# Cross attention with an adapter on one core: other ranks and other weights for changes of tiling in a build-time scheduler

## The chip, the core and the metric

The kernel runs on one core of a Trainium2 chip, in fp32. The metric is the time of one execution on the device in microseconds, smaller being better; a kernel's time is the median of its runs. Five engines work side by side, each through its own instructions in program order: TensorE (PE in the profile; PEld are its weight loads), VectorE (DVE), ScalarE (ACT), GpSimd (POOL) and SyncE (SP), which here issues the DMAs. They wait for each other by semaphores.

## The reference, cut to what matters

The inputs are x (2, 2048, 640) and a context (2, 128, 384). There are 8 heads of width 80. The last 4 tokens of the context belong to the adapter, the other 124 are text.

```python
query = hidden_states @ Wq                       # 2 x 2048 rows
keyt, valt = enc @ Wk, enc @ Wv                  # enc: 124 text tokens
hs = _mha(query, keyt, valt)
ca_q1 = jnp.einsum('btc,th->bch', ca, Wq_ca)     # 384 rows, from 4 tokens
ca_q1 = ca_q1[:, indices, :]                     # 2048 rows, each one of the 384
ca_hs1 = _mha(ca_q1, residual, residual)         # residual is x
ca_q2 = ca_hs1 @ Wq
ca_hs2 = _mha(ca_q2, ca @ Wk_ca, ca @ Wv_ca)
out = (hs + ca_hs2) @ Wout + b_out + residual
```

`_mha` is softmax attention with a scale of d ** -0.5. As the rows of ca_q1 repeat, everything behind them up to ca_hs2 is computed for 384 rows and gathered by index at the end.

## The kernel before, in words

**How it is issued.** Every part of the work is a Python generator (a task) that yields steps, `Do(engine, fn, after, needs, frees, marks, rank, mode)`: an engine or several to choose from, what must have ended, which rooms (buffers) are taken and freed. The class `Desk` (from L65) replays them while the kernel is built. It holds a clock of its own, fed by costs that are written in its methods (`matmul` L211, `transpose` L221, the others in `__getattr__` L236, `dma` L256), and at each turn issues the step that can start first; the program so made is kept in that order on every engine. The line numbers that the profile shows are mostly those of these helpers, so work is told by its tiles.

Among the steps that are ready at the same time on an engine, `run` takes the lowest sum of two numbers. One is `order`: the step's or its task's rank (small for what is wanted early) plus a correction for that single task, which stands in the table `RANKS` (L85) under the task's name and its count. The other is `change`: nothing if the step keeps TensorE's tiling or names none, `LEAVE` if TensorE is in the tiling of the whole array (128,128) and the step is in another, `SWITCH` if it goes from another to the whole one, `ANOTHER` if it goes between two smaller ones. Only some steps name their tiling (`mode=`): those of the queries, the text scores, the text values' weighting (`hidden`) and the output products. These weights act on the order alone. Where a step may go to several engines (`("POOL", "DVE", "ACT")`), the one that is free first takes it.

**The tilings.** A tiling (rows, columns) tells which part of TensorE's 128x128 array one product takes. The queries `pq` and the output products `po` use the whole; the text scores `sc` are (64,128), two side by side; the adapter's scores `s` are (32,128), four side by side; the adapter's sums `acc` and the text output `ph` are (128,32).

**The stages.** x is taken in 8 blocks of 512 rows, four in each batch b.

- Setup: weights are loaded and turned. `x_first` turns the first block on TensorE: for each of four groups of rows, `between` (L525 to 539) copies pieces of the row to `first_rows`, four pieces on VectorE, and one of 128x256 on ScalarE (L534); `turn` transposes them into `pt_x`, and copies go to `xt`. `z_weights` does the same with a small weight (`wqca_rest`). VectorE turns later blocks itself (`xt<-xi`).
- Queries: `queries` and, for later blocks, `queries_fast`, which forms sums of blocks and so needs fewer products. Parts of the queries go out to memory and come back (`away`, `landing`, `rests`).
- Adapter of a batch, `adapter(b)`: 24 steps of scores `s` into four banks of PSUM that only one step can hold, each followed by a VectorE maximum `mx` over 128x2048; then a chain over those maxima (`mt`, `pm`, `cop`); then 24 steps in which the scores are made again, ScalarE takes exponentials `ea`, and TensorE sums them up in `acc`; then the second attention, whose 384 rows `o2` go to memory.
- Text units m = 0 to 15 of 256 rows: scores `sc`, a softmax (maxima `m` on VectorE, exponentials `p` on ScalarE, the division `p<-p,r` on GpSimd, VectorE or ScalarE, of two halves of 128 rows each in one block or in eight activations), a turn `eb` on VectorE, a round trip through memory (`kept`, `pT`), `ph`, copies and sums `hs`, and chains of `po`, of which each result is added by VectorE to rows of x (`x_more` or `last_rows`). The rows of `o2` are added by an indirect DMA from GpSimd (L2047, `add_second`), ahead of or behind the products, and SyncE stores 128x640 rows. The last unit, 15, is stored in halves of 128x320.

Two batches follow one another, with text units between the adapter's steps wherever the ranks let them in; from about 480 us only text units are left.

Of the kernel before, what the change touches and what calls it, by code (L numbers as in the profile page):

```python
# [14 lines left out]
P = 128  # L15
# [49 lines left out]
class Desk:  # L65
# [1 line left out]


    ENGINES = ("PE", "ACT", "DVE", "POOL", "SP", "NONE")
    WHOLE, SWITCH, LEAVE, ANOTHER = (P, P), 15.7, 10.2, 10.9  # L70
    START = {(P, P): 0.107, (64, P): 0.143, (P, 64): 0.107, (64, 32): 0.1, (P, 32): 0.03}
    DRAIN = {
        ((P, P), (32, P)): 0.136, ((P, P), (64, P)): 0.035, ((P, P), (P, 64)): 0.056, ((P, P), (P, 32)): 0.067,
# [9 lines left out]


    RANKS = {  # L85
        "adapter": {1: 6},
        "chain": {8: -11, 9: -18, 14: -17, 15: -5, 19: -9, 20: 9, 24: -15, 29: 3, 31: -1, 32: 12.9, 35: 4, 36: 4,
            37: 4, 38: 4.3, 40: 5, 41: 3, 50: -11, 52: -5, 59: 10, 65: -8, 71: 11, 72: -2, 73: 8, 86: 10, 87: 10},
        "context": {0: -8},
        "contract": {1: 6, 2: 9, 3: 12},  # L90
        "halves_away": {0: -8, 1: -2, 3: -6, 4: 5, 6: -4},
        "probabilities": {0: -4, 1: 1.4, 3: 7, 4: 6, 7: -3, 8: -4, 12: 2, 15: 17},
        "queries": {0: -8},
        "queries_fast": {0: 10, 3: 12},
        "residual": {15: 3},
        "rest_back": {8: 7, 10: 12},
        "softmax": {1: -5, 3: -14, 10: -4, 12: -14, 13: -12, 21: 17, 24: 12, 26: 1.5, 29: 8},
        "stored": {5: -3},
        "sums_of_wq": {0: 2},
        "text_scores": {0: -3, 1: -2, 10: 5, 12: 4, 14: 6},  # L100
        "text_values": {0: 9},
        "values_weights": {0: 7},
        "x_load": {5: 11},
        "y_rows": {3: 11, 5: 9},
        "y_weights": {0: -3},
        "yz_block": {0: -11, 1: -11, 2: -4, 4: -6},
    }

    def __init__(self, tc):
# [153 lines left out]
def kernel(  # L263
# [14 lines left out]
    nc = tc.nc  # L278
# [25 lines left out]
    desk = Desk(tc)  # L304
# [220 lines left out]
    def between(to, t):  # L525

        pairs = t.rearrange("p (g d) -> p g d", g=2)
        kept = desk.spent
        desk.v_tensor_copy(to[:, 2 * R : P].rearrange("p (g d) -> p g d", g=2), pairs[:, :, D2 - VR : D2 + VR])
        upper = pairs[:, :, D2 + VR + VH :]  # L530
        exchanged = bass.AP(
            tensor=upper.tensor, offset=upper.offset, ap=[upper.ap[0], upper.ap[1], [-VH, 2], [1, VH]]
        )
        desk.pin(nc.scalar.copy(to[:, P : 3 * P].rearrange("p (g h d) -> p g h d", g=2, h=2), exchanged))  # L534
        desk.spent = kept
        desk.v_tensor_copy(to[:, R : 2 * R], t[:, 2 * D2 - VR : 2 * D2 + VR])
        desk.spent += 0.06656
        desk.v_tensor_copy(to[:, :VR], t[:, H - VR :])
        desk.v_tensor_copy(to[:, VR:R], t[:, :VR])
# [64 lines left out]
    def x_first():  # L604
# [8 lines left out]
        for k in range(4):  # L613
            yield Fork(one(Do(
                "DVE",
                lambda k=k: between(last[k], rows_of[0][:, k, :]),
                [("xrows", k)], marks=[("xlast", k)], rank=1,
            )), 1)
# [25 lines left out]
    def z_weights():  # L644

        rest = sp.tile([T, 3 * P], F32, name="wqca_rest")
        yield Do(
            "DVE",
            lambda: between(rest, wqca_sb),
            ["wqca"],  # L650
        )

        def turn(at):
            pw = bank(at[0], "pt_wqca")
            for c in range(NCH):
                transpose(pw[:, c * T : (c + 1) * T], rows_by_chunk(wqca_sb, rest, c), ident[:T, :T])
            return pw

        op = yield Do("PE", turn, needs=[(banks, 1)])
        yield Do(  # L660
            "DVE",
            lambda: desk.v_tensor_copy(wqcaT.rearrange("p c t -> p (c t)"), op.value[:, : NCH * T]),
            frees=[(banks, op.slots[0][0])],
        )
        yield Do(
            "DVE",
            lambda: spread_yz(
                wqcaT.rearrange("p (c x) t -> p c x t", x=1).to_broadcast([P, NCH, B, T]), Y
            ),
            marks=["wz"],  # L670
        )
# [1637 lines left out]
```

## Time and profile before

| | |
|---|---|
| median of 3 runs | 595.27 us (594.98, 596.28, 595.27) |
| the profiled execution | 595.79 us, its span 594.1 us |
| mean granted clock of TensorE | 1.00 |
| instructions | 12163 |
| busy: TensorE | 582.5 us (98%) |
| busy: VectorE | 388.6 us (65%) |
| busy: ScalarE | 321.3 us (54%) |
| busy: GpSimd | 135.3 us (23%) |
| chain that ended last | TensorE 66%, VectorE 16%, ScalarE 7%, DMA 6% |

The span is the time between the first and the last record of the profiled execution; that execution's time is 1.7 us more. Busy times come from records of instructions; the end of a matmul is modelled, so TensorE counts as busy also where it passes work on slowly. The chain that ended last follows the last instruction back to what released it, step by step.

### The profile page before, as it was taken

Reading aid. Unit: us, or ns where it says so; the run is one execution under the profiler, and the core shown is the slowest. Engines: PE = TensorE matmul, PEld = TensorE weight load, DVE = VectorE, ACT = ScalarE, POOL = GpSimd, SP = SyncE. Lnnn points to the kernel's source line nnn. Section 1 sums busy time; section 2 is a strip of 40 time slices with the busy share of each in tenths; the row PEclk is TensorE's granted clock in tenths of the full one; section 3 lists DMA queues with packets and bytes.
Section 4 is the critical chain, followed back from the end, with each engine's and each line's share of the span. In section 5 each row is a group of like instructions: output and inputs, shape, how many; then the busy total and the mean of one; then the engine's idle time right before and its main releaser. Section 6 shows DMA issues by size and latency. Waiting matters only on the chain.

```text
span 594.1 us, 12163 instructions
## 1 busy us (share of the span) xinstructions
PE 582.5 (98%) x4631; PEld 364.3 (61%) x4631; DVE 388.6 (65%) x633; ACT 321.3 (54%) x910; POOL 135.3 (23%) x197
## 2 busy tenths in 40 slices
PE   9999999999999999999999999999999999999997
PEld 7475456467766755555766566656555567666664
DVE  3247789999999565454989999975422253345343
ACT  3132345755777699999657583589667621101010
POOL 7202031143011521010005241250022022412241
PEclk9999999999999999999999999999999999999999
DMA  8997866694967675532899799898546948799986
GB/s 234 210 243 126 167 136 201 148 217 133 179 195 170 156 148 141 183 122 89 214 265 268 198 228 256 231 225 254 167 89 129 259 93 217 190 247 247 215 196 172
DMA packets 153011, 112.25 MB, mean 189 GB/s; under 512 B 83701, under 2 KB 126581, under 8 KB 152954
## 3 DMA queue, kind: packets, MB, share of 16 engines
q1 hardware_dynamic: 147322, 100.80, 65.8%
q0 software_dynamic: 5632, 10.69, 11.1%
q8 instruction: 36, 0.59, 0.4%
q14 instruction: 21, 0.17, 0.1%
HBM read 71.23 MB, written 40.22 MB: 188 GB/s over the span
## 4 chain that ended last, share of the span: by engine, by line
PE 66%; DVE 16%; ACT 7%; DMA 6%; issue 3%; SPq 1%; ACTq 0%; DVEq 0%
PE po L211 24%; PE pq L211 15%; PE acc L211 7%; DVE mx L236 6%; PE ph L211 6%; PE s L211 5%; ACT p L236 4%; PE sc L211 4%; DMA pT<-kept 3%; ACT ea L236 2%; PE pyz L211 2%; DVE m L236 2%; DVE eb L236 2%; DMA out_dram<-x_more 1%; PE pv L211 1%
## 5 line engine op out<-in xcount | busy, mean ns | idle before, releaser
L236 DVE TENSOR_REDUCE mx<-s 128x4 f32<-128x2048 f32 x48 | 109.2, 2275 | 7.2 <-PE s L211 7.0
L236 ACT ACTIVATE ea<-s 128x2048 f32<-128x2048 f32 x48 | 90.6, 1888 | 20.3 <-PE s L211 20.0
L236 ACT ACTIVATE p<-sc,m 128x124 f32<-128x124 f32 x256 | 89.8, 376 | 7.8 <-DVE m L236 7.3
L211 PE MATMUL pq<-xt,wq_sb 128*128 128x256 f32 (+1 forms) x272 | 86.1, 451 | 0.4 <-DVE q L236 0.2
L211 PE MATMUL po<-wout_sums,hs 128*128 128x320 f32 x256 | 79.2, 439 | 0.0
L211 PE MATMUL po<-wout_sb,hs 128*128 128x320 f32 x232 | 73.4, 442 | 0.3 <-DVE hs L236 0.2
L211 PEld LDWEIGHTS pq<-xt,wq_sb 128*128 128x128 f32 x272 | 49.1, 190 | 27.8 <-issue 18.4
L211 PEld LDWEIGHTS po<-wout_sums,hs 128*128 128x128 f32 x256 | 46.9, 190 | 22.9 <-issue 4.4
L236 DVE TENSOR_TENSOR x_more<-x_more,po 128x320 f32<-128x320 f32 x64 | 30.7, 481 | 44.4 <-PE po L211 43.9
L236 DVE TENSOR_TENSOR last_rows<-last_rows,po 128x320 f32<-128x320 f32 x64 | 30.8, 483 | 41.3 <-PE po L211 40.0
L211 PEld LDWEIGHTS po<-wout_sb,hs 128*128 128x128 f32 x232 | 42.2, 189 | 23.6 <-issue 4.8
L236 ACT COPY hs<-ph 128x512 f32<-128x512 f32 (+1 forms) x32 | 17.3, 556 | 72.3 <-PE ph L211 72.2
L236 ACT ACTIVATION_READ_ACCUMULATOR p<-sc,m 128x1 f32 x256 | 56.2, 219 | 0.0
L211 PE MATMUL acc<-ea,y_sb 128*32 128x384 f32 (+2 forms) x768 | 51.4, 385 | 0.0
L236 ACT ACTIVATE p<-p,r 128x124 f32<-128x124 f32 x136 | 41.2, 385 | 15.1 <-DVE r L236 15.1
L211 PE MATMUL ph<-pT,vpad 128*32 128x256 f32 x768 | 46.1, 381 | 0.5 <-issue 0.5
L236 DVE TENSOR_REDUCE m<-sc 128x4 f32<-128x496 f32 x64 | 40.4, 663 | 8.6 <-PE sc L211 8.6
L2047 POOL DMA_INDIRECT x_more<-o,query x16 | 24.8, 1550 | 90.8 <-DVE x_more L236 58.0
L236 DVE STREAM_TRANSPOSE eb<-p 128x1024 f32<-128x1024 f32 x32 | 39.4, 1232 | 3.0 <-DMA kept<-eb 1.5
L2047 POOL DMA_INDIRECT last_rows<-o,query x16 | 24.8, 1550 | 69.7 <-DVE last_rows L236 67.9
L211 PE MATMUL pq<-xt,wq 128*128 128x512 f32 x80 | 39.5, 612 | 0.0
L211 PEld LDWEIGHTS sc<-kmain,q 64*128 64x128 f32 x512 | 31.4, 187 | 12.0 <-issue 7.6
(214 smaller groups left out, 812.3 us busy)
## 6 DMA issues: line engine op xcount, KB each, us to landing
kept<-eb SPq DMA_DIRECT2D x32, 512.0 KB, 3.3
pT<-kept SPq DMA_DIRECT2D x64, 256.0 KB, 6.5
landing<-away SPq DMA_DIRECT2D x60, 128.0 KB, 3.7
xi<-in_x_dram SPq DMA_DIRECT2D x56, 128.0 KB, 3.9
x_more<-in_x_dram SPq DMA_DIRECT2D x16, 320.0 KB, 6.1
last_rows<-in_x_dram SPq DMA_DIRECT2D x16, 320.0 KB, 7.7
out_dram<-last_rows SPq DMA_DIRECT2D x16, 320.0 KB, 5.7
out_dram<-x_more SPq DMA_DIRECT2D x14, 320.0 KB, 8.8
```

The source lines that it names most:

```text
L211: self.pin(self.nc.tensor.matmul(out, lhsT, rhs, **kw))
L236: self.pin(getattr(engine, what)(*args, **kw))
L2047: desk.pin(nc.gpsimd.indirect_dma_start(out=t, out_offset=None, in_=o2_of[b], in_offset=bass.IndirectOffsetOnAxis(ap=query[:, st : st + 1] ...
```

## The change

All of it is numbers, but for one line. `LEAVE` goes from 10.2 to 19.7, `ANOTHER` from 10.9 to 25.1, and `SWITCH` from 15.7 to 122.8, more than any difference of ranks. The table `RANKS` is written anew: 130 single tasks get another correction, mostly chains of output products, softmax tasks, text scores, the adapter's sums, and parts of the first blocks. And the copy at L534 goes from ScalarE to VectorE; the desk's clock is set back behind it (`desk.spent = kept`) as before, so in that clock it still costs nothing.

```diff
-    WHOLE, SWITCH, LEAVE, ANOTHER = (P, P), 15.7, 10.2, 10.9
+    WHOLE, SWITCH, LEAVE, ANOTHER = (P, P), 122.8, 19.7, 25.1
...
     RANKS = {
-        "adapter": {1: 6},
-        "chain": {8: -11, 9: -18, 14: -17, 15: -5, 19: -9, 20: 9, 24: -15, 29: 3, 31: -1, 32: 12.9, 35: 4, 36: 4,
-            37: 4, 38: 4.3, 40: 5, 41: 3, 50: -11, 52: -5, 59: 10, 65: -8, 71: 11, 72: -2, 73: 8, 86: 10, 87: 10},
-        "context": {0: -8},
-        "contract": {1: 6, 2: 9, 3: 12},
-        "halves_away": {0: -8, 1: -2, 3: -6, 4: 5, 6: -4},
-        "probabilities": {0: -4, 1: 1.4, 3: 7, 4: 6, 7: -3, 8: -4, 12: 2, 15: 17},
-        "queries": {0: -8},
-        "queries_fast": {0: 10, 3: 12},
-        "residual": {15: 3},
-        "rest_back": {8: 7, 10: 12},
-        "softmax": {1: -5, 3: -14, 10: -4, 12: -14, 13: -12, 21: 17, 24: 12, 26: 1.5, 29: 8},
-        "stored": {5: -3},
-        "sums_of_wq": {0: 2},
-        "text_scores": {0: -3, 1: -2, 10: 5, 12: 4, 14: 6},
-        "text_values": {0: 9},
+        "adapter": {1: 1.2},
+        "chain": {6: -10, 7: 13, 8: 0.4, 10: 5, 11: 14, 12: 2.8, 13: 3, 15: -6, 19: -7, 21: -3, 22: -3, 23: -1,
+            27: 1, 28: -4, 29: -2, 30: -3, 32: 2.7, 34: -13, 36: -5, 37: -6, 41: 3, 42: 7, 44: -13.2, 45: -13.2,
+            46: -13.2, 47: -13.2, 48: -4, 50: -5, 52: -7.4, 53: -6, 56: 0.6, 57: 0.6, 59: 12, 61: -1, 69: 1.2,
+            70: 1.4, 72: -1, 76: -8, 83: 6, 84: -1},
+        "context": {0: -3},
+        "contract": {0: 4, 1: 5, 2: 4, 3: 1},
+        "halves_away": {1: -8, 3: -10, 4: 4.1, 5: 4, 6: 8},
+        "probabilities": {0: 3, 3: 9, 4: -3, 5: -3, 7: 5, 9: 9, 11: 2, 15: 4},
+        "queries": {0: -5},
+        "queries_fast": {0: 7, 1: 7, 2: 1, 3: 4, 5: -7},
+        "residual": {9: 8},
+        "rest_back": {3: 9, 8: 12},
+        "softmax": {1: -2, 2: -0.7, 3: -8, 6: -3, 8: -3, 9: -9, 10: -1, 11: -1, 12: -4, 13: -2, 21: 2, 22: -1,
+            23: 6, 24: -7, 25: -3, 28: 1, 29: 6, 30: 5},
+        "sums_of_wq": {0: 9},
+        "text_scores": {0: -13, 8: -14, 9: -11, 10: -11, 13: 11},
...
-        "x_load": {5: 11},
-        "y_rows": {3: 11, 5: 9},
-        "y_weights": {0: -3},
-        "yz_block": {0: -11, 1: -11, 2: -4, 4: -6},
+        "x_load": {1: -1},
+        "y_rows": {2: -1, 3: 10, 4: 7, 7: 3},
+        "y_weights": {0: 0.4},
+        "yz_block": {0: -5, 1: -4, 2: -3, 6: 2, 7: 2},
     }
...
     def between(to, t):
-        desk.pin(nc.scalar.copy(to[:, P : 3 * P].rearrange("p (g h d) -> p g h d", g=2, h=2), exchanged))
+        desk.v_tensor_copy(to[:, P : 3 * P].rearrange("p (g h d) -> p g h d", g=2, h=2), exchanged)
         desk.spent = kept
```

What the change does to the work shows in the orders that it produces, which are listed per engine: the same instructions on TensorE, in another order, and some small steps on other engines.

## The prediction

> **What bounds the kernel now.** I read the head of the page first, then the shares of the chain that ended last, and then busy time by stretches, which I cut where the adapter's steps begin and end.
>
> ```profile
> span 594.1 us, 12163 instructions
> ...
> PE 582.5 (98%) x4631; PEld 364.3 (61%) x4631; DVE 388.6 (65%) x633; ACT 321.3 (54%) x910; POOL 135.3 (23%) x197
> ...
> PE 66%; DVE 16%; ACT 7%; DMA 6%; issue 3%; SPq 1%; ACTq 0%; DVEq 0%
> ```
>
> TensorE is busy 582.5 of 594.1 us, so 11.6 us of idle time is all that better timing alone could remove; more than that must come out of TensorE's own work. The chain leaves TensorE for a third of its length, though, and the stretches say where. In each row stand the length, then busy time of PE, PEld, DVE, ACT and POOL.
>
> ```profile
> 100.00:120.00 20.00, 18.93 (x135) 11.56 (x134) 18.52 (x28) 13.53 (x51) 2.84 (x2) 1.00 0.66 159
> 120.00:145.00 25.00, 24.68 (x160) 17.27 (x159) 25.00 (x32) 14.50 (x59) 8.94 (x7) 1.00 0.76 200
> 145.00:170.00 25.00, 25.00 (x191) 17.79 (x189) 24.72 (x30) 15.75 (x59) 2.50 (x2) 1.00 0.82 174
> 170.00:192.00 22.00, 20.59 (x149) 14.08 (x148) 21.79 (x32) 17.82 (x73) 3.81 (x3) 1.00 0.66 161
> ...
> 230.00:280.00 50.00, 48.72 (x541) 28.36 (x535) 25.86 (x41) 47.37 (x98) 3.02 (x4) 1.00 0.39 124
> 280.00:310.00 30.00, 29.13 (x178) 20.15 (x178) 27.20 (x37) 19.61 (x74) 0.00 (x0) 1.00 0.90 221
> 310.00:340.00 30.00, 29.44 (x237) 18.96 (x239) 29.99 (x34) 17.43 (x70) 10.88 (x9) 1.00 0.93 247
> 340.00:370.00 30.00, 30.00 (x242) 18.93 (x242) 29.68 (x32) 18.49 (x78) 9.92 (x11) 1.00 0.95 232
> 370.00:400.00 30.00, 29.27 (x271) 18.22 (x270) 25.60 (x41) 21.05 (x71) 12.89 (x12) 1.00 0.89 223
> ...
> 480.00:594.00 114.00, 110.42 (x674) 73.21 (x672) 48.00 (x104) 13.50 (x28) 30.80 (x20) 1.00 0.85 205
> ```
>
> The granted clock, the third number from the end of each row, is 1.00 throughout and plays no part. VectorE is as full as TensorE from 100 to 192 (90.03 of 92 us) and from 280 to 370 (86.87 of 90): these are the two times 24 score steps, each of which ends in a maximum over 128x2048. ScalarE is full from 230 to 280 (47.37 of 50), where the exponentials of the same steps run. The idle time of TensorE in the nine rows ahead of the last is 1.07, 0.32, 0, 1.41, 1.28, 0.87, 0.56, 0 and 0.73, together 6.24 us. From 480 on TensorE alone counts: its 3.58 us of idle time lie almost wholly at the end, where the last stores land.
>
> **The change part by part.** The orders of the two kernels hold the same 2778 TensorE instructions with the same counts of each form. What differs is which stand next to each other, on which engine some small steps run, and when. A step that runs in another tiling than the one before it costs TensorE a pause, and by the two listings there are 311 such changes of tiling before and 295 after. By the tiling that is left: (128,128) 102 and 96; (128,32) 72 and 62; (64,128) 32 and 32; (64,32) 8 and 8; (32,128) 97 and 97.
>
> **The price of one change** I take from uninterrupted stretches of the chain of waits and from two rows of the timeline (start, length, what).
>
> ```profile
> 18.60 6.87 PE pq L211 x16
> ...
> 486.66 28.75 PE po L211 x106
> 515.40 5.32 PE ph L211 x96
> ...
> 563.58 2.73 PE ph L211 x48
> 566.30 11.50 PE po L211 x42
> ```
>
> ```profile
> 100.31 0.51 PE L211 MATMUL s<-zop,cop 32*128 32x512 f32 x4
> ...
> 100.75 1.15 PE L211 MATMUL sc<-kmain,q 64*128 64x124 f32 x15
> ```
>
> Between 96 and 48 passes of ph, in (128,32), lie 2.59 us: 0.054 a pass; 48 passes are 2.59, and 2.73 was taken, so leaving (128,32) cost 0.14 us. Between 106 and 42 passes of po, in (128,128), lie 17.25 us: 0.2695 a pass; 42 are 11.32 of 11.50, so leaving (128,128) cost 0.18 us. Leaving (32,128) cost nothing: four passes of 512 columns side by side began at 100.31, the next tiling at 100.75, and the 0.44 between is one such pass by the row of pq (6.87 / 16 = 0.43). The change thus takes away 6 x 0.18 + 10 x 0.14 = **-2.5 us** of TensorE time. [...] Were all of one price, the 311 changes would share what the rows of (128,128) and (128,32) alone give, 102 x 0.18 + 72 x 0.14 = 28.4 us, 0.09 each, and 16 fewer would bring -1.5 us; the rows at 100.31 and 100.75 speak against it.
>
> **Idle time that goes.** The normalisation of a block of probabilities is done in turn by ScalarE (eight activations), VectorE or GpSimd (one instruction).
>
> ```profile
> L236 ACT ACTIVATE ea<-s 128x2048 f32<-128x2048 f32 x48 | 90.6, 1888 | 20.3 <-PE s L211 20.0
> ...
> L236 ACT ACTIVATE p<-p,r 128x124 f32<-128x124 f32 x136 | 41.2, 385 | 15.1 <-DVE r L236 15.1
> ...
> L236 DVE TENSOR_REDUCE mx<-s 128x4 f32<-128x2048 f32 x48 | 109.2, 2275 | 7.2 <-PE s L211 7.0
> L236 DVE TENSOR_REDUCE m<-sc 128x4 f32<-128x496 f32 x64 | 40.4, 663 | 8.6 <-PE sc L211 8.6
> L236 DVE STREAM_TRANSPOSE eb<-p 128x1024 f32<-128x1024 f32 x32 | 39.4, 1232 | 3.0 <-DMA kept<-eb 1.5
> L236 DVE TENSOR_TENSOR p<-p,r 128x992 f32<-128x992 f32 x8 | 9.5, 1192 | 0.3
> ```
>
> In the listing after, VectorE does 11 of the 32 blocks instead of 8 and ScalarE 14 instead of 17. Beside the first batch's exponentials two blocks come to VectorE: unit 14's from ScalarE, where eight activations take 2.4 us, and unit 13's from GpSimd.
>
> ```profile
> 183.26 2.42 ACT p L236 x8
> ```
>
> With start-to-start times of the same forms ScalarE's work between the third and the twelfth of these 24 exponentials falls from 31.8 to 28.9 us, where TensorE has 31.7: ScalarE is then no longer the later one, and the 1.28 us of 230:280 should go. The VectorE it moves to is at 25.86 of 50 there, so 1.19 each is covered; without that cover it would cost up to 2.4. In the first VectorE stretch the listing gives VectorE 4.4 us less (120.3 to 115.9 from the first to the last maximum but one: three to four transposes of x are done earlier) and TensorE 1.9 us more (100.8 to 102.7). That should fill part of the 2.80 us idle in the first four rows; the 1.41 of 170:192 belongs to the chain of transposes behind the last maximum and stays, so I take half of the rest, -0.7. For the second stretch I take nothing. Together **-2.0 us**; the bounds are none (or a loss, the rivals) and -5.0, which is the nine rows' 6.24 less what the chains behind the last maxima hold.
>
> **The copy at L534** goes from ScalarE to VectorE, behind VectorE's own first copy of the same rows instead of beside it.
>
> ```profile
> 7.95 0.41 ACT L534 COPY first_rows<-xz 128x256 f32<-128x256 f32 x1 [0.71 <-DMA xz<-in_x_dram]
> 7.95 0.44 DVE L236 COPY first_rows<-xz 128x64 f32<-128x64 f32 x4 [1.18 <-DMA xz<-in_x_dram]
> ...
> 8.41 0.55 PE L221 MATMUL pt_x<-ident,first_rows 128*128 128x128 f32 x3
> ```
>
> Five copies move, four of rows and one of a weight. VectorE took 0.44 for its share, ScalarE 0.41 beside it; in a row that is some 0.8, so TensorE's transposes of the fourth row, at 8.41 now, start up to 0.4 later. The first three rows have transfers or transposes still to wait for. The following copies out of PSUM may take up a part: between 0 and +0.4, taken as **+0.2 us**.
>
> **The end.** Before, one unit's last rows run alone at the end and go out as half stores. In the listing after, unit 9 is interleaved with unit 15 there, and its last product stands 16 instructions (32 passes, 8.6 us) ahead of TensorE's last.
>
> ```profile
> 580.14 1.54 POOL L2047 DMA_INDIRECT last_rows<-o,query  x1 [0.30 <-DVE hs L236]
> ...
> 588.82 2.49 SPq L256 DMA_DIRECT2D out_dram<-x_more  x3
> 590.46 0.49 DVE L236 TENSOR_TENSOR x_more<-x_more,po 128x320 f32<-128x320 f32 x1 [1.13 <-PE po L211]
> ```
>
> ```profile
> last_rows<-o,query POOLq DMA_INDIRECT x3, 6.1
> ```
>
> The last row is from the view of the DMAs after 574: what it moves, how it is issued, how often, and the median of the us to landing. A unit's rows go through GpSimd's gather (1.54 us and 0.3 to the next, 6.1 to land by the median), then through a full store. Two of unit 9's gathers follow each other some 8 us ahead of the end: 8.1 - 1.8 - 6.1 lands within a microsecond of TensorE's end, about as the last add. On SyncE's queue the last full store of unit 9 now stands behind the half store that waits for that add. A full store has twice the bytes of the half store that ends now, and is one issue later, 2.49 / 3 = 0.8 at the most. I take **+1.0 us**, between +0.5 and +2.5 (the gather lands late, and the store with it).
>
> The sum against the profiled execution (595.79, span 594.1): -2.5 - 2.0 + 0.2 + 1.0 = **-3.3 us**, 592.5. That execution is 0.5 over the median of the runs, 595.27; the forecast for the median is **592.0**.
>
> **Rivals.** *VectorE decides the second stretch, and the kernel is slower.* From the second to the last maximum of the second batch the listing gives VectorE 89.0 us instead of 85.8: one more transpose eb (1.23), two more maxima m (0.66 each) and one more 128x512 step fall into it, while TensorE has 89.5 instead of 91.5. VectorE's slack in 280:370 was 3.13 us. If that slack cannot be used, because the maxima come in turns with TensorE through one PSUM quarter, the stretch lengthens by up to 3.2 us while 2.0 us of TensorE's work has gone elsewhere: 5.2 us more idle time. -3.3 + 5.2 = +1.9: 597.2. It decides from the point where VectorE's start-to-start total passes TensorE's; by count they are 0.5 apart. For it speaks the full VectorE in 310:340, against it that TensorE still has more. Chance 0.18.
>
> *Savings inside VectorE's stretches turn into waits, and nothing moves.* If about half of the 16 changes lie between 100 and 192 or 280 and 370, half of the 2.5 us is waited away again, no idle time goes, and the end costs 1.2: -1.25 + 1.2, 595.2. Chance 0.12.
>
> *All changes of tiling cost alike*, by the even price above: -1.5 instead of -2.5, 593.0. This is on the same side and lies within the forecast's range; chance 0.1 of its 0.70.
>
> *The copy or the order does not do what it says*: the listing shows it done, no chance is set aside.
>
> **How the numbers follow.** About 0.2% (1.2 us) is what a measurement of this kernel can tell from no change. Forecast with the even price: 0.70, faster by over 0.2% (below 594.1); no move 0.12; slower 0.18 (above 596.5). The range: the lowest is -2.5 - 5.0 + 0.7 with the cheap end, 588.5. The highest takes in no move and the lower end of the first rival, 596.8; what lies beyond, the rest of that rival, is some 0.15. The forecast's own range is 588.5 to 594.1.
>
> **What would show it.** Right: TensorE's busy time falls by some 2 to 3 us; in the stretch of the first batch's exponentials ScalarE is below its 47 of 50 and TensorE without idle time; uninterrupted rows of ph and po still give 0.14 and 0.18 a change. The first pq starts at most 0.4 later. The last store is a full one, issued behind the last add. Wrong: TensorE's idle time in the second stretch of maxima grows by over 3 us (the first rival), or the span's end lies over 5 us behind TensorE's last product (the gather).

## The result: slower by 1.3%, outside the range

The changed kernel takes **603.47 us** (median of 4 runs, 601.51 to 605.43) where the kernel before takes 595.70 (median of 4, 594.98 to 596.28): a ratio of 1.0131, 95% interval 1.0094 to 1.0168. Forecast were 592.0 us and a range up to 596.8. Each experiment below was timed beside runs of the kernel before of its own, whose median lies between 595.4 and 596.1 us. One run of experiment 5, of 608.29 us, more than 1.5% above the fastest of its kernel, is left out as slow. The profiled execution took 601.51 us, the fastest of the four, with a span of 599.8 against 594.1.

The head of the page after, and the chain that ended last:

```profile
span 599.8 us, 12140 instructions
...
PE 581.7 (97%) x4631; PEld 366.0 (61%) x4631; DVE 395.6 (66%) x645; ACT 313.4 (52%) x879; POOL 136.0 (23%) x195
...
PE 60%; DVE 21%; ACT 6%; DMA 5%; SPq 4%; issue 3%; DVEq 0%; ACTq 0%
```

TensorE is busy 0.8 us less than before, and idle 6.5 us more (18.1 against 11.6). VectorE's share of the chain grew from 16 to 21%. The stretch from 48 to 74, where the trouble begins, before the change:

```profile
48.00:74.00 26.00, 26.00 (x137) 12.51 (x129) 19.70 (x26) 8.96 (x25) 0.39 (x4) 1.00 0.81 158
```

The same stretch after it, and five of those of the prediction:

```profile
48.00:74.00 26.00, 22.92 (x132) 10.87 (x117) 16.56 (x25) 5.89 (x18) 1.30 (x13) 0.93 0.94 184
...
230.00:280.00 50.00, 49.78 (x570) 28.23 (x572) 27.58 (x44) 46.69 (x96) 3.03 (x4) 1.00 0.43 138
280.00:310.00 30.00, 28.00 (x185) 19.15 (x174) 24.71 (x34) 18.85 (x70) 2.90 (x2) 1.00 0.87 211
310.00:340.00 30.00, 27.86 (x216) 18.84 (x214) 29.78 (x30) 14.51 (x53) 9.05 (x8) 1.00 0.89 247
340.00:370.00 30.00, 29.19 (x234) 17.42 (x231) 28.61 (x34) 18.79 (x77) 10.16 (x11) 1.00 0.83 214
370.00:400.00 30.00, 29.00 (x226) 18.79 (x228) 27.55 (x38) 19.20 (x73) 10.02 (x10) 1.00 0.77 200
```

Three things stand there. From 48 to 74 TensorE is idle for 3.08 us, where it had no idle time at all, and its granted clock is 0.93 instead of 1.00. From 230 to 280 its idle time is 0.22 instead of 1.28, as forecast. And from 280 to 400 it is idle 5.95 us instead of 2.16. The view of TensorE's waits (what waits, for whom: us, times, longest) names the largest:

```profile
PE pvca L212 <- DMA w_vca<-in_L_xattn_Wv_ca_dram: 3.0, 1, 3.0
PE s L212 <- DVE mx L237: 3.0, 5, 1.3
PE pt_p L222 <- DVE q L237: 1.8, 1, 1.8
```

What follows the first of them shows in stretches of 2 us; the third number from the end of a row is the granted clock:

```profile
58.00:60.00 2.00, 0.79 (x2) 0.00 (x0) 1.74 (x1) 0.00 (x0) 0.00 (x0) 1.00 0.97 324
60.00:62.00 2.00, 0.18 (x4) 0.21 (x8) 0.00 (x0) 0.00 (x0) 0.00 (x0) 0.93 1.05 267
62.00:64.00 2.00, 2.00 (x28) 1.21 (x23) 0.00 (x0) 0.29 (x2) 0.00 (x0) 0.50 1.24 248
64.00:66.00 2.00, 2.00 (x7) 0.88 (x4) 1.57 (x1) 0.20 (x2) 0.00 (x0) 0.72 0.74 74
```

TensorE stands for 3.0 us, and then works at half its clock for some 3 us more (0.50 from 62 to 64, 0.72 from 64 to 66). In experiment 1 the clock fell to 0.50 behind a stand of 2.1 us, while behind one of 2.9 us in experiment 5 it stayed at 1.00. So stands of nearly the same length cost the clock in one execution and not in another, and what decides it no run shows. The spread of this kernel's runs, 3.9 us against 1.3 before, fits that.

Without the time at the lower clock TensorE's work has become shorter, as forecast: in two kernels of experiments 4 and 5 that have all 295 changes of tiling, and a clock of 1.00 in the profiled execution, it is busy 579.8 and 579.9 us against 582.5 before. A saving of the forecast size, 2.5 us, came; idle time took more than that back.

### The profile page after: what moved, and what is told of

The parts are those of the page before. It is cut to its first block, busy times and chain, and to the rows that moved or that the text cites. A ratio compares the mean times of both kernels' runs of the same rounds, so it can differ in the third digit from the quotient of the medians.

```text
span 599.8 us, 12140 instructions
## 1 busy us (share of the span) xinstructions
PE 581.7 (97%) x4631; PEld 366.0 (61%) x4631; DVE 395.6 (66%) x645; ACT 313.4 (52%) x879; POOL 136.0 (23%) x195
## 4 chain that ended last, share of the span: by engine, by line
PE 60%; DVE 21%; ACT 6%; DMA 5%; SPq 4%; issue 3%; DVEq 0%; ACTq 0%
PE po L212 22%; PE pq L212 14%; DVE mx L237 9%; PE acc L212 6%; PE ph L212 6%; PE s L212 4%; SPq L257 4%; ACT p L237 4%; DMA kept<-eb 3%; PE sc L212 3%; DVE eb L237 2%; ACT ea L237 2%; DVE m L237 2%; DVE q L237 1%; PE pyz L212 1%
## 5 line engine op out<-in xcount | busy, mean ns | idle before, releaser
L237 ACT ACTIVATE ea<-s 128x2048 f32<-128x2048 f32 x48 | 90.8, 1891 | 20.0 <-PE s L212 19.7
L212 PE MATMUL po<-wout_sb,hs 128*128 128x320 f32 x248 | 77.1, 439 | 0.2
L237 DVE TENSOR_TENSOR x_more<-x_more,po 128x320 f32<-128x320 f32 x80 | 38.3, 482 | 57.0 <-PE po L212 56.1
L212 PEld LDWEIGHTS po<-wout_sums,hs 128*128 128x128 f32 x256 | 46.7, 190 | 25.1 <-issue 6.2
L2048 POOL DMA_INDIRECT x_more<-o,query x20 | 31.1, 1557 | 135.9 <-DVE x_more L237 106.5
L212 PEld LDWEIGHTS po<-wout_sb,hs 128*128 128x128 f32 x248 | 45.6, 190 | 22.2 <-issue 3.4
L237 ACT COPY hs<-ph 128x512 f32<-128x512 f32 (+1 forms) x34 | 18.7, 554 | 66.6 <-PE ph L212 66.6
L237 ACT ACTIVATE p<-p,r 128x124 f32<-128x124 f32 x112 | 33.9, 384 | 12.1 <-DVE r L237 11.9
L237 DVE TENSOR_TENSOR last_rows<-last_rows,po 128x320 f32<-128x320 f32 x48 | 23.0, 481 | 25.3 <-PE po L212 23.6
L212 PE MATMUL sc<-kmain,q 64*128 64x124 f32 x512 | 38.0, 284 | 0.3 <-DVE q L237 0.3
```

Source lines behind the costliest of these rows:

```text
L212: self.pin(self.nc.tensor.matmul(out, lhsT, rhs, **kw))
L237: self.pin(getattr(engine, what)(*args, **kw))
L2048: desk.pin(nc.gpsimd.indirect_dma_start(out=t, out_offset=None, in_=o2_of[b], in_offset=bass.IndirectOffsetOnAxis(ap=query[:, st : st + 1] ...
```

## The experiments

**1. The load that TensorE stood for.** The product p_kca ran at 35.1 us instead of 25.4. This comes from `RANKS`, where the correction of its task (`y_weights`) went from -3 to 0.4; its step names no tiling, so the weight of a change does not count for it. (Replayed without the chip, the desk makes the same orders up to 75 us of its clock with the old weights as with the new ones, by the old table and by the new: what the front loses comes from the table, and with `y_weights` alone put back p_kca is early again.) It frees the buffer of w_vca, whose load went out at 55.6 us instead of 29.9, behind 13 loads of x and eight of wout_sb on SyncE's queue. The edit issues it right behind p_kca and exchanges two buffers:

```diff
+    def early_vca():
+        w_c["vca"] = sp.tile([P, NCC, H], F32, tag=f"w{room_of['kca']}", name="w_vca")
+        desk.pin(nc.sync.dma_start(w_c["vca"], Wv_ca.rearrange("(c p) n -> p c n", p=P)))
...
-            "PE", lambda at: by_groups(at[0], "p2_kca", cadT, w_c["kca"]),
+            "PE", lambda at: (by_groups(at[0], "p2_kca", cadT, w_c["kca"]), early_vca())[0],
```

> The changed kernel with one DMA moved: the load of w_vca is issued right behind the product p_kca that frees its buffer (some 36 us) instead of at 55.6 us; the two buffers involved are swapped between w_vca and k_parts, every other instruction keeps its place. Theory A (TensorE's stand at 58.8 to 61.8 us, and the granted clock of 0.50 to 0.93 behind it, are lost for good): the stand goes, the clock stays at 1.00, 4.6 us less at least, 597 to 599 us, and a smaller spread between runs. Rival B (VectorE's maxima limit what follows, so the stand is waited off there anyway): TensorE's waits grow between 100 and 190 us instead, and the time stays above 601 us.

Measured: 602.63 us (6 runs, 600.53 to 607.27), 1.0128 times before (1.0098 to 1.0158). Theory A fell; but the reason is not B's. The timeline of VectorE and TensorE there:

```profile
55.10 0.71 DVE L237 STREAM_TRANSPOSE xt<-xi 128x512 f32<-128x512 f32 x1 [1.99 <-DMA xi<-in_x_dram]
...
58.58 1.02 PE L212 MATMUL pvca<-w_vca,caT 128*32 128x160 f32 x24
59.42 2.25 DVE L237 TENSOR_REDUCE mx<-s 128x4 f32<-128x2048 f32 x1
...
61.73 0.80 PE L212 MATMUL s<-zop,cop 32*128 32x512 f32 x4 [2.13 <-DVE mx L237]
```

pvca no longer waits. The next step of scores does, for the first maximum: on VectorE that stands behind five turns of x, and the first of these waits 2 us for its load. Mended in one place, the stand comes back in the next, 2.1 us instead of 3.0, and behind it the clock is again at 0.50:

```profile
62.00:64.00 2.00, 2.00 (x6) 0.86 (x7) 1.42 (x1) 0.00 (x0) 0.00 (x0) 0.50 0.62 205
```

B's waits between 100 and 190 did not come: TensorE is idle 2.6 us from 100 to 192, against 2.3 in the changed kernel.

**2. The copy alone.**

```diff
-        desk.pin(nc.scalar.copy(to[:, P : 3 * P].rearrange("p (g h d) -> p g h d", g=2, h=2), exchanged))
+        desk.v_tensor_copy(to[:, P : 3 * P].rearrange("p (g h d) -> p g h d", g=2, h=2), exchanged)
```

> The kernel before with only the copy of 128x256 (five times, at the start) on VectorE instead of ScalarE; nothing else moves. The prediction's term: 0 to +0.4 us, the first query product at most 0.4 us later. Rival: it is hidden by the transfers of x, no difference.

Measured: 595.68 (11 runs) beside 595.45, a ratio of 1.0004 (0.9996 to 1.0013): -0.2 to +0.8 us. The term of +0.2 stands, and so does nothing at all.

**3. Is VectorE the limit of the second stretch?** The 24 maxima of the second batch over half of their columns, in the kernel before and in the changed one with the early load:

```diff
-                        lambda q4=op.value: desk.v_tensor_reduce(mx[:, ct, u, :, sb], q4, AX.X, ALU.max),
+                        lambda q4=op.value: (half_of if b else desk.v_tensor_reduce)(
+                            mx[:, ct, u, :, sb], q4, *([] if b else [AX.X, ALU.max])
+                        ),
...
+    def half_of(to, q4):
+        desk.v_tensor_reduce(to, q4[:, :, :256], AX.X, ALU.max)
...
```

> The kernel before, with the 24 maxima of the second batch over half of their keys (the rest is left out), which takes some 1.1 us off VectorE in each; the order is the same. If VectorE is what TensorE waits for in the second stretch of maxima (281 to 400 us), most of the 3.3 us of TensorE's waits there go: 591.5 to 593 us. If transfers or PSUM are what it waits for, under 1 us goes.

> The same cut of the second batch's maxima (half of the keys left out) in the changed kernel with the early load. If the changed kernel loses its time in the second stretch because VectorE has more to do there than TensorE (the prediction's first rival), its 7.9 us of waits from 281 to 400 us fall to what the kernel before has with the same cut, and its time comes some 5 to 6 us below that of the early load alone, to about the time of the kernel before with the cut. If something else holds TensorE up there (the round trip of the probabilities, GpSimd), 3 us or more of the waits stay.

Measured, one run each: 594.11 and 595.78 us. The kernel before gains 1.3, less than the 2 us forecast at the least; the changed one gains 6.8. The distance of 7.2 us between them shrinks to 1.7, so 5.5 us would hang on VectorE in the second stretch; but the runs of the early load alone lie 6.7 us apart, and one run with the cut tells the size only roughly. The traces are firmer: TensorE's waits from 280 to 402, added up from the view of waits, are 2.1 us before, 5.7 after and 6.1 with the early load; with the cut 1.2 and 1.3. So VectorE is the limit, and the 3.6 us by which the waits had grown shrink to 0.1. From the second to the last maximum of this batch, before and after:

```profile
290.40:379.51 89.11, 88.43 (x671) 56.49 (x669) 86.38 (x94) 52.45 (x204) 25.16 (x24) 1.00 0.94 233
```

```profile
289.76:385.03 95.27, 90.05 (x677) 57.81 (x676) 91.29 (x100) 55.39 (x215) 25.80 (x25) 1.00 0.88 226
```

Before, TensorE is busier than VectorE, 88.4 against 86.4 us; after, VectorE is, 91.3 against 90.1.

**4. Which stretch costs what.** To take the stretches apart, the desk was made to issue a written list of steps:

```diff
     def run(self):
-        while any(self.queue.values()):
...
+        for step in LINED.split():
+            engine, path = step[0], step[1:]
...
+            self.issue(max(ready, self.free[e], self.now), e, found[0])
```

A list is joined from both kernels: the steps of one up to a time of the desk's clock, then all others in the order of the other kernel.

> From here the steps are issued from a written list, so that one stretch can be taken from one kernel and the rest from the other; at the two cuts, 100 and 260 us of the desk's clock, both kernels have done the same steps, but for three or four. This one: the kernel before up to 100 (its copy at L534 on ScalarE included), the changed kernel from there on. Theory A (the front costs 4 to 5 us by TensorE's stand and the slow clock, whatever it waits for): 598 to 599.5 us, clock 1.00. Rival B (what is lost in front comes back later): above 601.5 us.

> The changed kernel up to 100, the kernel before from there on. Theory A: 599.5 to 600.5 us, with the stand and a granted clock below 1.00 between 58 and 66 us. Rival B: within 1.5 us of the kernel before.

> The kernel before up to 100, the changed kernel from 100 to 260 (the first batch's maxima and exponentials), the kernel before from there on. The prediction's gains of the first half should stand alone here: ScalarE's idle 1 us and about half of the fewer changes of tiling, 592.5 to 594 us. If it is within 0.5 us of the kernel before, the gain of the first half was only work moved to a later place.

> The kernel before up to 260, the changed kernel from there on (the second batch's maxima, exponentials and the end). Theory A, with the prediction's first rival at 5.5 us (from the pair with half of the maxima: 6.8 less 1.3) and 0.9 for the end, against 1 to 1.5 us of fewer changes: 599.5 to 601 us, with TensorE's waits behind the maxima between 285 and 400 us. If the second stretch suffers only because the front brings it out of step, under 597 us.

| up to 100 | 100 to 260 | from 260 | us, median | ratio to before, 95% | changes of tiling |
|---|---|---|---|---|---|
| before | before | before | 595.80 | | 311 |
| after | before | before | 601.39 | 1.0096 (1.0082 to 1.0111) | 311 |
| before | after | before | **593.49** | 0.9960 (0.9948 to 0.9973) | 309 |
| before | before | after | 599.02 | 1.0054 (1.0041 to 1.0067) | 297 |
| before | after | after | 597.31 | 1.0024 (1.0012 to 1.0036) | 295 |
| after | after | after | 603.47 | 1.0131 (1.0094 to 1.0168) | 295 |

The front costs 5.6 us, the middle brings 2.3, the last part costs 3.2: together +6.5, and measured were 7.8 (against the 595.70 of its own runs). The front cost 0.9 us more than had been expected of it at the most, the last part 0.5 less than at the least; the signs were right. None of the 16 fewer changes of tiling lies in the front, 2 in the middle and 14 in the last part, where by its trace eight of them fall between 280 and 400. The last part has both in it: in its profiled execution TensorE is busy 1.6 us less than before, and idle 4.4 us more.

**5. What the front loses by.** From the list of the changed kernel, with the early load (one name for each step): the first scores and the first maximum ahead, a product pv between the two steps of scores.

```diff
 PE    pyz, pv, pv,
-      pv, s, pq, pq, pvca, s
+      s, pq, pv, pq, pvca, s
 DVE   zop,
-      xt, zs, xt, xt, zop, xt, xt, mx, mx
+      mx, zs, xt, zop, xt, xt, xt, mx, xt
```

(xt, zs and zop are the turns of x, the shuffle and the second copy of z; the first maximum is the mx that comes first in each row.)

> The changed kernel from a written list, with a few steps of the first 60 us moved, nothing else: the load of w_vca behind p_kca; the first step of scores ahead of the last of four products pv, that pv behind the first query product after it; on VectorE the first maximum ahead of the five turns of x instead of behind them, the second ahead of the last turn. Theory A (the order of the front makes TensorE stand: products of the whole array are bunched ahead of the first scores, and the maximum that the second scores wait for is queued behind turns that wait for loads): no stand between 55 and 66 us, granted clock 1.00, and the time of the kernel that has the front of before, 597 to 598 us. Rival B (the loads of x themselves are too late, whatever the order): a stand of 2 us or more remains, over 600 us.

Measured: 601.77 (6 runs, 600.14 to 605.81), 1.0111 (1.0082 to 1.0139). The stand at 58 us was gone and the clock of the profiled execution 1.00, as A had it; yet the time hardly moved, as B had it. Both are wrong as stated, since what waits is now later:

```profile
70.32 2.27 SPq L431 DMA_DIRECT2D k_parts<-k_away  x4
...
76.08 1.02 ACT L411 CAST krest<-k_parts 128x992 fp32r<-128x992 f32 x1 [6.60 <-DMA k_parts<-k_away]
77.13 0.71 DVE L411 STREAM_TRANSPOSE yt<-yz 128x512 f32<-128x512 f32 x1 [3.78 <-ACT krest L411]
...
84.33 1.56 PE L386 MATMUL pq<-x_sums,wq_sums 128*128 128x256 f32 x6 [0.64 <-DVE wq_sums L411]
```

ScalarE stands 6.6 us for the key rests' round trip through memory, VectorE 3.8 us behind ScalarE, and TensorE at 83 to 89 behind both, 2.3 us in all. The loads that end the trip went out at 70.3 us, behind nine loads of x; before, behind two, they went out at 66.7:

```profile
63.27 0.43 SPq L256 DMA_DIRECT2D k_away<-k_parts  x1
63.81 0.65 SPq L256 DMA_DIRECT2D xi<-in_x_dram  x1
64.91 0.61 SPq L1102 DMA_DIRECT2D xi<-in_x_dram  x1
66.73 1.74 SPq L256 DMA_DIRECT2D k_parts<-k_away  x4
```

So those four loads were moved, with and without the other mend (which has the early load of w_vca in it):

```diff
 SP    k_away, xi, xi,
-      xi, xi, xi, xi, xi, xi, xi, k_parts x4
+      k_parts x4, xi, xi, xi, xi, xi, xi, xi
```

> The changed kernel with only those four loads moved. Theory C: the stand at 58 us is still there, so no gain, 602 to 604 us. Rival (the key rests alone are what the front loses by): 597 to 599 us.

> The mended front of before, and on SyncE the four loads k_parts<-k_away moved ahead of the loads of x numbered 2 to 5 of the next block, as the kernel before has them; nothing else. Theory C (the front has two late chains that end within a few tenths of each other: scores and maxima, and the key rests' round trip, held on SyncE's queue behind loads of x): both are mended, TensorE does not wait between 50 and 100 us, 597 to 598 us. Rival (a third limit, the transfers themselves): over 600 us.

| | key loads late | key loads early |
|---|---|---|
| scores and maxima as changed | 603.47 | 602.94 |
| scores and maxima mended | 601.77 | **597.88** |

Each mend alone brings 0.5 or 1.7 us, which the spread of these kernels' runs, 4 to 7 us, does not tell from nothing; both bring 5.6 (1.0033 times before, 1.0021 to 1.0046), which is what the front costs. TensorE is then busy all the time from 54 to 62 and 80 to 90:

```profile
58.00:62.00 4.00, 4.00 (x35) 1.93 (x34) 3.56 (x4) 0.94 (x3) 0.00 (x0) 1.00 0.69 206
...
80.00:90.00 10.00, 10.00 (x77) 5.35 (x76) 7.24 (x12) 5.87 (x21) 0.00 (x0) 1.00 0.30 97
```

The runs with only the key loads early went from 599.01 us at a mean clock of 0.999 to 605.67 at 0.992. The first is the profiled one: TensorE stands for 2.9 us there, and its clock stays at 1.00 (the rows from 58 to 66):

```profile
58.00:62.00 4.00, 1.06 (x25) 0.73 (x24) 1.22 (x1) 0.00 (x0) 0.00 (x0) 1.00 1.06 269
62.00:66.00 4.00, 4.00 (x23) 1.58 (x15) 2.36 (x2) 0.94 (x3) 0.00 (x0) 1.00 0.76 136
```

That the others stood as long and lost some of theirs is likely, by the changed kernel's trace, but no trace of them is kept.

**6. What the last part loses by.** In the changed order VectorE has a difference of 640 columns and zop where GpSimd makes its sums of the output weights; before, a maximum stood in zop's place. VectorE and GpSimd in the kernel with the changed last part:

```profile
321.03 1.46 DVE L410 TENSOR_TENSOR wout_sums<-wout_sb 128x640 f32<-128x640 f32 x1
322.42 2.04 DVE L410 SCALAR_TENSOR_TENSOR zop<-zop,low_z,zb 128x512 fp32r<-128x512 f32 x1
324.38 2.28 DVE L410 TENSOR_REDUCE mx<-s 128x4 f32<-128x2048 f32 x1
```

```profile
320.26 1.55 POOL L410 TENSOR_TENSOR wout_sums<-wout_sb 128x640 f32<-128x640 f32 x1 [12.17 <-PE pq L385]
321.89 3.97 POOL L410 TENSOR_TENSOR wout_sums<-wout_sb,wout_sums 128x640 f32<-128x640 f32 x2
```

zop takes 2.04 us. The same GpSimd steps, three in number, were replaced in both kernels by copies on ScalarE, which leave the subtraction out:

```diff
-                (desk.g_tensor_tensor if desk.engine == "POOL" else desk.v_tensor_tensor)(t[:, i], x, y, ALU.subtract)
+                if desk.engine == "POOL":
+                    return desk.a_copy(t[:, i], x)
+                desk.v_tensor_tensor(t[:, i], x, y, ALU.subtract)
```

> The kernel with the changed kernel's last part (behind 260), with the three subtractions that GpSimd does for wout_sums between 320 and 326 us replaced by copies on ScalarE (the subtraction is left out in these three). VectorE's zop at 322.4 took 2.04 us beside them, 0.71 elsewhere. Theory A (VectorE steps are stretched by GpSimd's beside them, and that is a part of what the last part loses): zop back to 0.7, 597.5 to 598.2 us. Rival B (VectorE's own order and number of steps alone): within 0.4 us of 599.0.

> The kernel before with the same three subtractions of GpSimd replaced by copies on ScalarE (left out). There a maximum of 2.28 us, as long as elsewhere, ran beside them on VectorE, where the changed kernel has zop (2.04 instead of 0.71). Theory A (the place decides: what VectorE runs beside GpSimd): within 0.6 us of the kernel before. Rival (GpSimd's sums cost 1.8 us wherever they stand): 594 to 594.4 us.

Measured: 597.20 (11 runs) where the last part as changed gave 599.02, and 594.91 (12 runs) where before gave 595.61 (0.9989, 0.9976 to 1.0001). 1.8 and 0.7 us: the second lies between the two forecasts for it, and the difference, some 1 us, would be what the place of GpSimd's sums costs; with intervals of some 0.7 us on either side of each median it is not clear of the noise. In the first, TensorE's waits for the maxima from 280 to 402 fell from 2.1 to 0.5, and zop was back to 0.75 and the difference to 0.82, while the maximum takes as long as it did:

```profile
321.86 0.82 DVE L410 TENSOR_TENSOR wout_sums<-wout_sb 128x640 f32<-128x640 f32 x1
322.60 0.75 DVE L410 SCALAR_TENSOR_TENSOR zop<-zop,low_z,zb 128x512 fp32r<-128x512 f32 x1
323.26 2.29 DVE L410 TENSOR_REDUCE mx<-s 128x4 f32<-128x2048 f32 x1
```

So zop takes 2.04 us beside GpSimd's sums and 0.75 without them, the difference 1.46 and 0.82, but the maximum behind them 2.28 and 2.29. In the kernel before, a maximum that runs beside the sums from its start to its end takes 2.28 as well:

```profile
320.81 2.28 DVE L236 TENSOR_REDUCE mx<-s 128x4 f32<-128x2048 f32 x1
```

```profile
320.28 3.65 POOL L236 TENSOR_TENSOR wout_sums<-wout_sb,wout_sums 128x640 f32<-128x640 f32 x2
```

By the kernel zop and the difference read two pieces of SBUF each, the maximum one of PSUM; whether that is what tells them apart, no run shows.

Two attempts to win it back by order alone, one exchange on VectorE and one on TensorE:

```diff
 DVE
-      wout_sums, zop, mx
+      wout_sums, mx, zop
```

> The kernel with the changed kernel's last part, with two neighbours on VectorE exchanged: the maximum (2.28 us) ahead of zop, so that the maximum stands beside GpSimd's sums. Nothing left out. Theory A: zop takes 0.7 to 1.3 us, TensorE's 1.3 us of waiting for that maximum goes, 597.5 to 598.3 us. Rival (VectorE is only full there): within 0.4 us of 599.0.

```diff
 PE
-      s, pt_p, pq, po, pq
+      s, pq, pt_p, pq, po
```

> The kernel with the changed kernel's last part, with two steps of the second attention on TensorE (the turn pt_p, which waits 1.8 us for VectorE, and the product behind it) moved behind the next query products, which are ready. Theory A (VectorE decides this stretch): the wait goes, and comes back behind the next maxima, within 0.5 us of 599.0. Rival (the step is only misplaced on TensorE): 1.3 to 1.8 us less, 597.2 to 597.7.

Measured: 599.22 and 599.09 us (6 runs each), no gain in either. The trace of the first shows part of the reason: behind the maximum zop still takes 1.46 us, and a division p after it 1.63 instead of 1.18. Of the 0.58 us that zop gains, 0.45 is lost there. In the second, the 1.8 us of waiting for pt_p goes, and waits of the products behind it take its place: 5.6 us in all from 280 to 402, against 5.5. That VectorE's total sets the pace fits both, and leaves little for an order that only exchanges neighbours.

**7. The price of a change of tiling.** Forty lone products added behind output products near the end of the kernel before:

```diff
+                    if m in (11, 12, 13, 14, 15):
+                        desk.pin(nc.tensor.matmul(
+                            to[:, HALF : HALF + P], ident[:32, :], ident[:32, :],
+                            start=False, stop=True, skip_group_check=True,
+                        ))
```

> The kernel before with 40 added products of 32 rows x 128 columns, 128 wide, in the units 11 to 15, one behind each output product, into PSUM columns that nobody reads. Each costs its two passes (0.22 us by the row of 128 columns, if a pass takes as long in this tiling) and two changes of tiling: leaving (128,128), 0.18, and leaving (32,128). By the prediction's prices, in which the latter is free: 40 x 0.40 = 16 us. Were every change 0.09: the same 16 us here, so this run is read against the next one.

> The same with 40 added products of 128 rows x 32 columns. By the prediction's prices, leaving (128,32) is 0.14 where leaving (32,128) is free: 5.6 us more than the run with 32 rows. If every change of tiling costs alike: no difference.

Measured: 619.19 and 616.24 us (2 runs each) beside 596.10, 0.58 and 0.50 us a product. The order of the two is the reverse of the forecast. The timeline with 32 rows, then with 32 columns:

```profile
559.85 0.48 PE L2160 MATMUL po<-ident 32*128 32x128 f32 x2
560.26 0.81 PE L211 MATMUL po<-wout_sb,hs 128*128 128x320 f32 x2
561.00 0.48 PE L2160 MATMUL po<-ident 32*128 32x128 f32 x2
```

```profile
560.23 0.41 PE L2160 MATMUL po<-ident 128*32 128x128 f32 x2
560.57 0.81 PE L211 MATMUL po<-wout_sb,hs 128*128 128x320 f32 x2
561.30 0.41 PE L2160 MATMUL po<-ident 128*32 128x128 f32 x2
```

From start to start the two passes of po take 0.74 and 0.73, against 0.54 by the prediction's 0.2695 a pass: leaving the whole array costs 0.20. The two added passes take 0.41 and 0.34; by the 0.43 of the prediction for a pass of 512 columns, two of 128 would be 0.22, so by this estimate leaving (32,128) costs 0.19 and leaving (128,32) 0.12, behind a lone product. Behind the kernel's own scores, four products side by side, the price of (32,128) is still not seen, also where the whole array comes next (in the kernel before):

```profile
142.16 0.51 PE L211 MATMUL s<-zop,cop 32*128 32x512 f32 x4
142.60 1.78 PE L211 MATMUL pq<-xt,wq_sums 128*128 128x256 f32 x7
```

These are 0.44 us for one pass of 0.43; in 46 of the 48 such places the next step starts 0.43 or 0.44 us behind the scores, whatever its tiling. So a change around a lone product costs an estimated 0.12 to 0.20 us, and behind the scores none of it shows.

**8. The best of the parts.**

> The front with both mends, the changed kernel's middle up to 260, the kernel before from there on. If the mended front loses nothing and keeps its few changes of tiling less, 593 to 593.7 us, level with the kernel that has the front of before (593.5).

Measured: 593.61 us (6 runs, 593.18 to 593.95), 0.9958 (0.9944 to 0.9973), level with the 593.49 of the kernel with the front of before. Both beat the kernel before by 0.4% and the changed one by 1.6%.

## Why the prediction was wrong, point by point

**The price of the tiling.** This term came out, in size. The prices of leaving (128,128) and (128,32), 0.18 and 0.14, were measured at 0.20 and 0.12; that of leaving (32,128), nothing, holds for the scores from which it was read, though not behind a lone product, and its count is 97 in both kernels. Where the clock stayed at 1.00, TensorE's busy time fell by 2.6 and 2.7 us, for 2.5 forecast. Part by part it is not shown to be the changes of tiling: the middle alone has 1.0 us less where two changes fewer give 0.3, the last part 1.6 where 14 give 2.2, and executions of the kernel before and of those with its order differ by up to 0.6 (581.9 to 582.5). What failed is the rest of the sum: idle time grew by more than this term saved.

**The idle time.** ScalarE's term was right in its place: idle time from 230 to 280 fell by 1.06 us of 1.28. The other 0.7 of the forecast 2.0 did not come: with the changed middle alone TensorE is idle 2.77 us from 100 to 192, against 2.80. That this middle brings 2.3 us, near the forecast 2.0, is in part luck: in its profiled execution 1.1 us of it are idle time, and 1.0 is busy time that only two changes of tiling less do not explain.

**The first 100 us.** This is the step that failed most, and it was not a term too small but one that was missing. The prediction compared the counts of TensorE's steps and of its changes of tiling, and let the front cost only the copy. It did not follow what the new ranks move ahead (three products pv in a row, which had filled the pauses between the scores) and what they move back: p_kca by 10 us, with it the buffer, with the buffer a load on SyncE's queue; and it did not read SyncE's and VectorE's queues for which loads now stand ahead of which. Price: 5.6 us, of two chains that end at about the same time, the slow clock behind the stand counted in.

**The second stretch.** Here the forecast took nothing, and this failed too. The first rival had the place and the mechanism: VectorE's total passes TensorE's, 91.3 against 90.1 us, and TensorE's waits hang on VectorE's maxima. It also named the sign, over 3 us more idle time in this stretch: from 280 to 400 they are 3.8 more. It had the size too large, 5.2. The forecast gave it 0.18, because TensorE's count was still 0.5 us above VectorE's. Two totals within 0.5 us of each other in 89, with all steps in turns through one PSUM room, are no margin; and VectorE's steps were counted by their durations from before, which the new neighbours on GpSimd lengthened: one zop took 2.04 us instead of 0.75.

**The end.** Forecast were +1.0 us, with a full store as the last. From the last add's end to the span's end there are 3.2 us before (590.95 to 594.1) and 4.0 after:

```profile
592.04 4.58 SPq L257 DMA_DIRECT2D out_dram<-x_more  x6
...
595.29 0.49 DVE L237 TENSOR_TENSOR x_more<-x_more,po 128x320 f32<-128x320 f32 x1 [1.12 <-PE po L212]
```

That is 0.9, right by the profiled executions; no run takes the end apart from the rest.

**What stays open:** the 1.3 us between the sum of the three parts and the whole. The whole has the lowest mean clock of the kernels in experiment 4's table (0.990 to 0.995), so that it may be the clock, but no run shows it. No run on the chip takes the new weights apart from the new ranks, so which of the two earns the middle and costs the last part is open as well.

## What to carry to other kernels

The same work in another order is not the same time: before counting what a new order saves on one engine, follow for each step that was put off which buffer it frees and which load waits for that buffer, and for each step that was put ahead which pause it used to fill. In a kernel whose first part lives on loads, compare the DMA queue's order before TensorE's. Where a mend brings nothing, look whether the wait has only moved to the next queue: two limits that end together must both be mended before either shows.

## What the runs showed of the hardware

A stand of TensorE can cost more than itself: behind 3.0 us in the changed kernel, and behind 2.1 us in that with the early load, the granted clock fell to 0.50 for some 3 us, while behind 2.9 us in that with the key loads early it stayed at 1.00. VectorE's zop took 2.04 us beside GpSimd's sums of the output weights and 0.75 without them, the difference of 640 columns 1.46 and 0.82, while a maximum over PSUM took 2.28 beside them and 2.29 without. A lone product in a small tiling costs TensorE 0.50 to 0.58 us between products of the whole array, of which an estimated 0.3 to 0.4 are the two changes; four scores side by side in (32,128) are followed by the next tiling after 0.44 us, one pass of 0.43.
